# Inputs laid out in DRAM field by field, and two other weight chunks loaded in two parts, in a kernel of bilinear field pairs on one Trainium2 core

## Chip, core and metric

The kernel runs on one core of a Trainium2 chip (trn2). The metric is the time of one execution on the device in microseconds (us); of several executions the median is given. A profile shows one further execution, with what each engine did: PE is the matrix engine, PEld its weight loads, DVE, ACT and POOL are the vector, scalar and GpSimd engines, and SP is the sync engine, which here only issues DMAs. Sixteen DMA engines move all data between DRAM and the core's SBUF.

## The reference

There are 1024 samples of 32 fields, each a vector of 128 numbers, in float32. For each of the 496 pairs of fields i < j there is a 128 x 128 matrix of weights. The output of a pair is the vector of field i times the matrix, multiplied elementwise by the vector of field j:

```python
v_i = inputs[:, I_IDX, :]
v_j = inputs[:, J_IDX, :]
transformed = jnp.einsum('bpd,ped->bpe', v_i, W)
return transformed * v_j
```

The inputs are 16.8 MB, the weights 32.5 MB, the output is 260 MB.

## The kernel before

**Work and order.** The pairs are worked through with i falling from 30 to 0 (`_pairs`), so field 0 is needed last, and only as the left factor. A pair q has two halves of 512 samples; a unit u is one half of one pair. For each unit PE multiplies into a bank of PSUM (`first`, line 197), and DVE multiplies the result by x_j into an output tile `ot` (line 222). For float32 accuracy a product is made of three matmuls of split operands: of x_i the parts xh, xl, xd, of the weights wh, wl, wd. Two matmuls (line 207) are followed by a scaling on ACT (line 208), then the third (line 216). The first 15 pairs use the unsplit operands (line 204). Weights are split two pairs at a time, a "chunk of two" (`split_w`, lines 128 to 136): ACT makes wh (line 133), then POOL makes wl and wd in three instructions (lines 134 to 136). The fields are split in the same way by `split_x`. The list `todo` gives each split the pair from which it may run, some five pairs before its use.

The program's order on each engine is written out by hand: the loop over u at line 231 emits the instructions, and each engine runs its own in that order. An instruction that waits holds up what is behind it on its engine. SP has nothing to do but issue loads, so it is ahead of the others and waits only for what each load needs. POOL issues loads too, but between its splits, in its order.

**Buffers.** Weights are loaded eight pairs at a time, 512 KB: w_c is the c-th of 62 such chunks. Three buffers (tag "w") hold them in turn, so a load must wait until the splits of an older chunk are done. Field 0 (x_0) takes one turn of these three buffers, between w_54 and w_55, and so w_57 gets the buffer in which x_0 was, once POOL has split x_0. Chunk c is asked for at the pair `w_at` (lines 181 to 185): 17 pairs ahead of its first pair, but for w_55, w_56 and w_57, which are asked for 11 pairs ahead (`XAFTER`). Output tiles hold four pairs (2 MB) and there are three; ACT's queue issues their stores (line 255), and DVE waits for a store before it writes that buffer again.

**Loads in two parts.** Most loads are one DMA of 128 rows on SP. Some are in two parts (`load_apart`, line 107): 112 rows are one DMA that POOL issues, its access written with 14 as the outer size and 8 as the inner one, and the last 16 rows are one DMA that SP issues. `move_on(k)` (line 103) has POOL issue a tiny read of 2k pieces of 64 bytes into the tile `mark`, with k as the outer size: k is 5 ahead of all, 2 three pairs after each load in two parts, and 13 after the last of them. Loaded in two parts are the fields 1 to 14, two at a time (`load_x_apart`), and the weight chunks in `WAPART`. The host reorders the 112 rows of these so that each lands in its partition.

**Layout of x in DRAM.** `xt` is [128 dimensions, 32 fields, 1024 samples]: a row of a field is 4 KB, the next row of the same field lies 128 KB on. `wt` is [62, 128, 8, 128], each chunk one block of 512 KB.

Of the kernel before, what the change touches and what calls it, by code (L numbers as in the profile page):

```python
# [7 lines left out]
F32 = mybir.dt.float32  # L8
# [3 lines left out]
P = 128  # L12
NF = 32
NQ = NF * (NF - 1) // 2
BT = 1024
HB = 512
WC = 2
WL = 8
# [16 lines left out]
NE = 14  # L35
ROWS = 8 * NE
XAPART = 14
XSTEP, XPOS = 4, 8
WAPART = (45, 47, 49, 51, 54, 57, 59)
BACK = 3  # L40
SLAG = 2

# [7 lines left out]
def kernel(  # L50
# [22 lines left out]
    nc = tc.nc  # L73
# [3 lines left out]
    xpool = ctx.enter_context(tc.tile_pool(name="x", bufs=1))  # L77
    spool = ctx.enter_context(tc.tile_pool(name="xs", bufs=2))
    rpool = ctx.enter_context(tc.tile_pool(name="wr", bufs=WB))
# [3 lines left out]

    x_sb = {}

    def load_x(f, n=1, pieces=1, eng=None):

        if f == 0:

            t = rpool.tile([P, WL, P], F32, tag="w", name="x_0").rearrange("p q e -> p (q e)").unsqueeze(1)  # L90
        else:
            t = xpool.tile([P, n, BT], F32, tag=f"x{f}", name=f"x_{f}")
        s = BT // pieces
        for k in range(pieces):
            (eng or nc.sync).dma_start(out=t[:, :, k * s : (k + 1) * s], in_=xt[:, f : f + n, k * s : (k + 1) * s])
        for k in range(n):
            x_sb[f + k] = t[:, k, :]

    w_raw = {}

    mark = xpool.tile([32, 16], F32, tag="mark", name="mark")

    def move_on(k):

        nc.gpsimd.dma_start(out=mark[: 2 * k], in_=xt[: 2 * k, 0, :16].rearrange("(b a) n -> a b n", a=k))  # L105

    def load_apart(dst, src):
        nc.gpsimd.dma_start(out=dst[:ROWS], in_=src[:ROWS].rearrange("(b a) m n -> a b m n", a=NE))  # L108
        nc.sync.dma_start(out=dst[ROWS:], in_=src[ROWS:])

    def load_x_apart(f):

        t = xpool.tile([P, 2, BT], F32, tag=f"x{f}", name=f"x_{f}")
        load_apart(t, xt[:, f : f + 2, :])
        for k in range(2):
            x_sb[f + k] = t[:, k, :]

    def load_w(c, splits=(0, WL), eng=nc.sync):
        w_raw[c] = rpool.tile([P, WL, P], F32, tag="w", name=f"w_{c}")
        if c in WAPART:  # L120
            load_apart(w_raw[c], wt[c])
            return
        for a, b in zip(splits, splits[1:]):
            eng.dma_start(out=w_raw[c][:, a:b, :], in_=wt[c, :, a:b, :])
# [44 lines left out]

    load_w(0, (0, 1, WL), nc.sync)  # L170
    load_x(NF - 2, pieces=2, eng=nc.scalar)
    load_x(NF - 1, pieces=2, eng=nc.scalar)
    load_x(NF - 3)
    load_x(NF - 4)
    load_w(1, eng=nc.sync)
# [55 lines left out]
    for u in range(2 * NQ + LAG + SLAG):  # L231
        q = u // 2
        if u < 2 * NQ:
            i, j = pairs[q]
            if u % 2 == 0 and j == i + 1 and XAPART < i - 2 - XLEAD:
                load_x(i - 2 - XLEAD)
            first(u)
            if u == 2 * nq0:
                move_on(5)
            f = i - XSTEP  # L240
            if u % 2 == 0 and 0 < f < XAPART and f % 2 == 1 and j == i + XPOS:
                load_x_apart(f)
                back.append(q + BACK)
            if u % 2 == 1 and q in w_at:
                load_w(w_at[q])
                if w_at[q] in WAPART:
                    back.append(q + BACK)
            if u % 2 == 0 and q in back:
                move_on(16 - NE if q < w_q[WAPART[-1]] else 13)
            if u == 2 * x_at + 1:  # L250
                load_x(0)
# [43 lines left out]
```

## Time and profile before

| | |
|---|---|
| median of 5 runs | 753.18 us (752.01 to 755.11) |
| the profiled execution's time | 751.63 us |
| its span, first to last instruction | 749.9 us |
| granted clock of PE, mean | 0.992 |
| busy: PE, DVE, ACT, POOL | 93%, 86%, 84%, 81% |
| moved by DMA | 310 MB, 413 GB/s over the span |
| ACT's queue (q10: the stores) and SP's (q1: loads) | 82.7% and 13.1% of the 16 engines' time |
| loads that POOL issues (q0) | 9.64 MB, 3.6% |

How to read it: the page cuts the span into 40 slices of 18.75 us and gives each engine's busy tenths in each, and what the DMA engines moved. "A waits for B" is put down where an engine was idle before an instruction, to what released it. In a timeline line stand the start, the duration, the engine, the line of the code, the operation with its tiles, and in brackets the idle time before it and what ended that. An idle engine costs nothing unless another one, or the end, waits for it.

### The profile page before, as it was taken

The page shows a single profiled execution, that of the slowest core. Times are in us where ns is not written, and L with a number is a line of the kernel's source. Part 1 is how long each engine was busy: PE and PEld are TensorE (multiplying, and loading weights), DVE is VectorE, ACT ScalarE, POOL GpSimd, SP SyncE. Part 2 cuts the span into 40 slices and gives each one's busy share as a digit, 9 for nine tenths or more (in the row PEclk, how much of TensorE's full clock was granted, in tenths as well). Part 3 has the DMA queues.
Part 4 walks back from the last instruction along what each step waited for, and adds up shares of the span by engine and source line. Part 5 has one row for each costly group of instructions (what it writes and reads, how often), then busy time and mean ns, then how long its engine had stood idle before and what let it go on. Part 6 is the DMA issues. An engine that isn't in the chain of part 4 may idle for free.

```text
span 749.9 us, 11008 instructions
## 1 busy us (share of the span) xinstructions
PE 698.8 (93%) x2946; PEld 550.4 (73%) x2946; DVE 643.1 (86%) x1012; ACT 627.0 (84%) x1256; POOL 611.1 (81%) x892
## 2 busy tenths in 40 slices
PE   7989999998999999989999998999999999997994
PEld 3567777776777777768777776877787877776883
DVE  4989999998888888889979888988888888896995
ACT  1388889998898889889888988988898998876993
POOL 1888999999999998978988887888888878785671
PEclk9999999999999999999999999999999999998998
DMA  9999999999999999999999999999999999997998
GB/s 354 429 423 427 428 426 413 419 387 425 426 408 431 404 426 424 423 427 426 420 410 425 431 410 431 416 414 407 426 417 424 416 428 396 429 417 298 425 425 350
DMA packets 32957, 310.05 MB, mean 413 GB/s; under 512 B 4480, under 2 KB 4608, under 8 KB 16384
## 3 DMA queue, kind: packets, MB, share of 16 engines
q10 hardware_dynamic: 19584, 261.10, 82.7%
q1 hardware_dynamic: 10816, 38.61, 13.1%
q0 software_dynamic: 2496, 9.64, 3.6%
q8 instruction: 24, 0.39, 0.2%
q14 instruction: 37, 0.30, 0.1%
HBM read 49.29 MB, written 260.05 MB: 413 GB/s over the span
## 4 chain that ended last, share of the span: by engine, by line
PE 60%; DMA 20%; POOL 13%; DVE 4%; issue 2%; ACT 0%; DVEq 0%; POOLq 0%; ACTq 0%
PE po L207 38%; PE po L216 18%; DMA out_dram<-ot 18%; PE po L204 4%; DVE ot L222 3%; POOL wl L134 3%; POOL xd L154 3%; POOL xl L149 3%; POOL wd L136 2%; DMA w<-in_wt_dram 2%; POOL xl L150 1%; POOL wd L135 1%; DMA x<-in_xt_dram 0%; ACT wh L133 0%; DVE xd L262 0%
## 5 line engine op out<-in xcount | busy, mean ns | idle before, releaser
L222 DVE TENSOR_TENSOR ot<-po,x 128x512 f32<-128x512 f32 x992 | 628.6, 685 | 98.4 <-DMA out_dram<-ot 47.6
L208 ACT ACTIVATE po<-po 128x512 f32<-128x512 f32 x962 | 545.0, 583 | 86.3 <-PE po L207 34.5
L207 PE MATMUL po<-xl,wl 128*128 128x512 f32 x962 | 377.6, 393 | 15.4 <-POOL wl L134 15.3
L207 PE MATMUL po<-xh,wh 128*128 128x512 f32 x962 | 378.5, 393 | 11.8 <-DVE ot L222 11.6
L216 PE MATMUL po<-xd,wd 128*128 128x512 f32 x962 | 375.8, 391 | 9.6 <-ACT po L208 6.3
L134 POOL TENSOR_TENSOR wl<-w,wh 128x256 fp32r<-128x256 f32 x241 | 180.7, 750 | 55.6 <-ACT wh L133 53.2
L207 PEld LDWEIGHTS po<-xh,wh 128*128 128x128 f32 x962 | 180.9, 188 | 60.5 <-DVE ot L222 22.1
L207 PEld LDWEIGHTS po<-xl,wl 128*128 128x128 f32 x962 | 181.0, 188 | 59.7 <-POOL wl L134 23.6
L216 PEld LDWEIGHTS po<-xd,wd 128*128 128x128 f32 x962 | 181.0, 188 | 49.2 <-issue 5.9
L136 POOL TENSOR_TENSOR wd<-wl,wd 128x256 fp32r<-128x256 f32 x241 | 178.5, 741 | 20.1
L135 POOL TENSOR_SCALAR wd<-wh 128x256 fp32r<-128x256 f32 x241 | 99.3, 412 | 20.5
L133 ACT ACTIVATE wh<-w 128x256 fp32r<-128x256 f32 x241 | 99.3, 413 | 12.2 <-DMA w<-in_wt_dram 7.1
L149 POOL TENSOR_TENSOR xl<-x,xh 128x512 fp32r<-128x512 f32 x52 | 67.3, 1294 | 18.9 <-ACT xh L148 18.6
L154 POOL TENSOR_TENSOR xd<-xh,xl 128x512 fp32r<-128x512 f32 x32 | 41.3, 1292 | 2.7
L148 ACT ACTIVATE xh<-x 128x512 fp32r<-128x512 f32 x52 | 32.5, 628 | 11.3 <-DMA x<-in_xt_dram 11.1
L150 POOL TENSOR_SCALAR xl<-xl 128x512 fp32r<-128x512 f32 x52 | 34.7, 668 | 4.6
L204 PE MATMUL po<-x,w 128*128 128x512 f32 x60 | 27.9, 625 | 4.3 <-DMA x<-in_xt_dram 4.2
L204 PEld LDWEIGHTS po<-x,w 128*128 128x128 f32 x60 | 11.6, 198 | 19.8 <-issue 12.5
L262 DVE TENSOR_TENSOR xd<-xh,xl 128x512 fp32r<-128x512 f32 x20 | 17.7, 885 | 0.0
L105 POOL DMA_DIRECT2D mark<-in_xt_dram x15 | 9.6, 640 | 0.0
L108 POOL DMA_DIRECT2D w<-in_wt_dram x7 | 4.4, 624 | 0.0
L108 POOL DMA_DIRECT2D x<-in_xt_dram x7 | 4.4, 623 | 0.0
(5 smaller groups left out, 1.7 us busy)
## 6 DMA issues: line engine op xcount, KB each, us to landing
out_dram<-ot ACTq DMA_DIRECT2D x122, 2048.0 KB, 11.6
w<-in_wt_dram SPq DMA_DIRECT2D x54, 512.0 KB, 10.3
x<-in_xt_dram SPq DMA_DIRECT2D x16, 512.0 KB, 9.7
x<-in_xt_dram POOLq DMA_DIRECT2D x7, 896.0 KB, 13.8
w<-in_wt_dram POOLq DMA_DIRECT2D x7, 448.0 KB, 11.7
out_dram<-ot ACTq DMA_DIRECT2D x6, 512.0 KB, 8.0
x<-in_xt_dram ACTq DMA_DIRECT2D x4, 256.0 KB, 5.8
out_dram<-ot ACTq DMA_DIRECT2D x4, 256.0 KB, 6.0
```

The costliest lines, as they stand in the source:

```text
L133: nc.scalar.mul(h, raw, 1.0 - 2.0**-13)
L134: nc.gpsimd.tensor_tensor(l, raw, h.bitcast(F32), ALU.subtract)
L135: nc.gpsimd.tensor_scalar(d, h.bitcast(F32), EPS, 1.0, ALU.mult, ALU.mult)
L136: nc.gpsimd.tensor_tensor(d, l.bitcast(F32), d.bitcast(F32), ALU.subtract)
L149: nc.gpsimd.tensor_tensor(l, x_sb[f][:, s], h.bitcast(F32), ALU.subtract)
L150: nc.gpsimd.tensor_scalar(l, l.bitcast(F32), 1.0 / EPS, 1.0, ALU.mult, ALU.mult)
L154: nc.gpsimd.tensor_tensor(d, h.bitcast(F32), l.bitcast(F32), ALU.subtract)
L204: nc.tensor.matmul(po[u], w_raw[q // WL][:, q % WL, :], x_sb[i][:, s], start=True, stop=True)
L207: nc.tensor.matmul(po[u], w_s[c][t][:, r], x_s[i][t][:, s], start=t == 0, stop=t == 1)
L208: nc.scalar.mul(po[u], po[u], 1.0 + EPS)
L216: nc.tensor.matmul(po[u], w_s[q // WC][2][:, r], x_s[i][2][:, s], start=False, stop=True, skip_group_check=True)
L222: nc.vector.tensor_tensor(ots[g][:, k, s], po.pop(u), x_sb[j][:, s], ALU.mult)
```

## The change

The host lays x out as [32 fields, 128, 1024], a field being one block of 512 KB; the fields that are loaded two at a time lie as one block of 1 MB for both, with a row of 8 KB (both fields) for each dimension. The loads' access patterns follow. `move_on` reads its few short pieces from field 0. And in `WAPART` 57 and 59 are exchanged for 58 and 60.

```diff
-WAPART = (45, 47, 49, 51, 54, 57, 59)
+WAPART = (45, 47, 49, 51, 54, 58, 60)
...
-            (eng or nc.sync).dma_start(out=t[:, :, k * s : (k + 1) * s], in_=xt[:, f : f + n, k * s : (k + 1) * s])
+            (eng or nc.sync).dma_start(out=t[:, k * s : (k + 1) * s], in_=xt[f, :, k * s : (k + 1) * s])
...
-        nc.gpsimd.dma_start(out=mark[: 2 * k], in_=xt[: 2 * k, 0, :16].rearrange("(b a) n -> a b n", a=k))
+        nc.gpsimd.dma_start(out=mark[: 2 * k], in_=xt[0, : 2 * k, :16].rearrange("(b a) n -> a b n", a=k))
...
-        load_apart(t, xt[:, f : f + 2, :])
+        rows = xt[f : f + 2].rearrange("m d b -> (m d b)").rearrange("(d m b) -> d m b", m=2, b=BT)
+        load_apart(t, rows)
...
-    xt = _np.ascontiguousarray(x.transpose(2, 1, 0))
-    late = xt[:ROWS, 1 : XAPART + 1].reshape(NE, 8, XAPART, BT)
-    xt[:ROWS, 1 : XAPART + 1] = late.transpose(1, 0, 2, 3).reshape(ROWS, XAPART, BT).copy()
+    xt = _np.ascontiguousarray(x.transpose(1, 2, 0))
+    for f in range(1, XAPART, 2):
+
+        two = xt[f : f + 2].transpose(1, 0, 2).copy()
+        two[:ROWS] = two[:ROWS].reshape(NE, 8, 2, BT).transpose(1, 0, 2, 3).reshape(ROWS, 2, BT).copy()
+        xt[f : f + 2] = two.reshape(2, P, BT)
```

More of the change, by code (lines that the diff above doesn't have):

```diff
@@ L84, with load_x @@
     x_sb = {}
-    def load_x(f, n=1, pieces=1, eng=None):
+    def load_x(f, pieces=1, eng=None):
         if f == 0:
-            t = rpool.tile([P, WL, P], F32, tag="w", name="x_0").rearrange("p q e -> p (q e)").unsqueeze(1)
+            t = rpool.tile([P, WL, P], F32, tag="w", name="x_0").rearrange("p q e -> p (q e)")
         else:
-            t = xpool.tile([P, n, BT], F32, tag=f"x{f}", name=f"x_{f}")
+            t = xpool.tile([P, BT], F32, tag=f"x{f}", name=f"x_{f}")
         s = BT // pieces
         for k in range(pieces):
-            (eng or nc.sync).dma_start(out=t[:, :, k * s : (k + 1) * s], in_=xt[:, f : f + n, k * s : (k + 1) * s])
-        for k in range(n):
-            x_sb[f + k] = t[:, k, :]
+            (eng or nc.sync).dma_start(out=t[:, k * s : (k + 1) * s], in_=xt[f, :, k * s : (k + 1) * s])
+        x_sb[f] = t
     w_raw = {}
```

## The prediction, made before the changed kernel ran

> **What bounds the kernel now.** I read the page's slices first, then the waits of the stretch that stands out, then its timeline, then busy sums and DMA rates stretch by stretch. From the page:
>
> ```profile
> PE   7989999998999999989999998999999999997994
> DMA  9999999999999999999999999999999999997998
> GB/s 354 429 423 427 428 426 413 419 387 425 426 408 431 404 426 424 423 427 426 420 410 425 431 410 431 416 414 407 426 417 424 416 428 396 429 417 298 425 425 350
> ```
>
> The sixteen DMA engines are full from the first microseconds, at about 420 GB/s, and PE is nearly full too. Transfers are the tighter limit of the two. One slice of 18.75 us, the 37th (675 to 694 us), falls to 298 GB/s and to 7 tenths. Apart from the first and the last it is the only real hole. The waits from 660 us to the end:
>
> ```profile
> POOL wl L134 <- ACT wh L133: 18.1, 19, 5.8
> DVE ot L222 <- PE po L216: 7.4, 4, 6.0
> ACT wh L133 <- DMA w<-in_wt_dram: 6.6, 1, 6.6
> PE po L216 <- ACT po L208: 5.5, 1, 5.5
> ```
>
> One wait of 6.6 us of ACT for a weight load, and every other engine then waits 5.5 to 6 us for ACT. The timeline says which load:
>
> ```profile
> 663.94 0.74 POOL L134 TENSOR_TENSOR wl<-w,wh 128x256 fp32r<-128x256 f32 x1
> ...
> 665.93 0.62 POOL L108 DMA_DIRECT2D w<-in_wt_dram  x1
> ...
> 669.56 2.50 ACT L208 ACTIVATE po<-po 128x512 f32<-128x512 f32 x4
> ...
> 678.63 0.42 ACT L133 ACTIVATE wh<-w 128x256 fp32r<-128x256 f32 x1 [6.58 <-DMA w<-in_wt_dram]
> ```
>
> ACT is done at 672.05 and wants the first pair of w_57. Chunk 57 is loaded in two parts. SP issued its 16 rows at 657.92 (5.5 us to landing), as soon as the buffer was free; POOL's 112 rows stand in POOL's own order behind splits, and were issued only at 665.93; they took 12.5 us and landed at 678.5. ACT's queue is in order: the products of earlier pairs (L208) stand behind the waiting wh. What the stall costs, by stretches:
>
> ```profile
> core 0: us, PE busy (x) PEld busy (x) DVE busy (x) ACT busy (x) POOL busy (x), PEclk, DMA share, GB/s
> 678.00:683.00 5.00, 3.32 (x8) 2.67 (x9) 1.38 (x2) 3.66 (x8) 3.29 (x6) 0.50 0.31 129
> 683.00:686.00 3.00, 3.00 (x15) 2.40 (x13) 2.79 (x5) 2.41 (x6) 1.63 (x3) 0.96 0.87 360
> 686.00:690.00 4.00, 4.00 (x19) 3.34 (x18) 4.00 (x6) 3.61 (x8) 2.97 (x6) 1.00 1.12 326
> 690.00:726.00 36.00, 36.00 (x161) 29.80 (x160) 36.00 (x54) 33.45 (x68) 25.19 (x41) 1.00 1.00 421
> 726.00:738.00 12.00, 12.00 (x55) 9.93 (x54) 12.00 (x19) 10.82 (x21) 5.65 (x9) 1.00 0.94 393
> 738.00:748.00 10.00, 1.92 (x8) 1.03 (x6) 3.50 (x6) 1.17 (x3) 0.00 (x0) 0.83 0.99 397
> ```
>
> The last two columns are DMA share and rate. Transfers go on a while from what is queued, then run dry from 678 to 683 us. From 690 us PE and DVE never wait again, though DVE waited 8 times, 8.4 us in all, for stores between 560 and 665 us: the stall emptied the store queue (store landing 11.9 us median before it, 8.4 after).
>
> **The change part by part. (1) w_57 becomes one plain load on SP.** SP issues it where it now issues the 16 rows, at 657.92, since the wait is for the same buffer (which x_0 held until POOL had split it). Six plain weight loads issued between 560 and 670 us took 10.0 to 11.9 us. So w_57 lands at 667.9 to 669.8, 2.2 us or more before 672.05. The stall goes. For PE that is 5.5 us of idle, and the slow clock after it: in the chain of waits nine matmuls from 679.68 to 683.64 take 3.95 us, where nine take 2.04 us later (0.68 us for three), so 1.9 us more; 7.4 us in all. For the DMA, by bytes: 678 to 690 us moved 5 x 129 + 3 x 360 + 4 x 326 = 3.03 MB, which at the 421 GB/s of the next stretch takes 7.2 us, not 12: 4.8 us. In 726 to 738 us the queues were thin (393 GB/s): 4.72 MB at 421 take 11.2 us, another 0.8. DMA gains 5.6 us, PE 7.4. What is late next is the store queue, so the smaller one holds. Store waits of about 1 us come back (8.4/8), and while one lasts PE can be short of work when the queue is next free; I take off 0.6 us, about half of one. **Minus 5.0 us.**
>
> **(2) w_58 becomes a two-part load.** Its POOL issue (0.62 us, as now, only moved) comes one split of three instructions after w_57's place: 665.93 + 2.0 = 668.0. Queued behind it on POOL are the splits, delayed by what w_57's no longer costs, so nothing net. POOL's weight loads take 7.4/11.7/13.9 us (least, median, most), POOL's loads of both kinds at most 15.1. It lands at 679.7, at most 681.9. ACT wants it four pairs' cadence of 2.72 us after 672.05, at 682.9. Spare: 3.2 us, at least 1.0. Cost nothing; with 15.1 us it would be 0.2 us late. Its 16 rows on SP (7.1 us at most) are issued at about 662.7, where the full load is now.
>
> **(3) w_59 becomes plain, w_60 two-part.** w_59 is issued by SP at about 672 and wanted at 672.05 + 8 x 2.72 = 693.8: far ahead. w_60's POOL issue is 16 pairs after w_58's, 668.0 + 21.8 = 689.8, and wanted at 704.6: 14.8 us for a load of 11.7. Nothing, at most 0.3 us late with 15.1. The two kinds stay at seven loads each; the two tiny reads into mark (0.63 us of POOL each) only move along.
>
> **(4) Fields as blocks.** No instruction, byte or row length changes: a field still arrives in rows of 4 KB, a pair in rows of 8 KB; in DRAM a field's rows lie 4 KB apart, a pair's 8 KB, instead of 128 KB. The layout of before can be priced against w, which already lies in blocks. POOL's queue q0 carries only pairs of fields from 155 to 514 us, only weights from 516 to 700 us (besides the small reads):
>
> ```profile
> q0 software_dynamic: 1157, 6.18, 4.8%
> q0 software_dynamic: 1274, 3.26, 5.0%
> ```
>
> Columns: packets, MB, share of 16 engines. The first is 0.048 x 359 / 6.18 = 2.79 us per MB, the second 0.050 x 184 / 3.26 = 2.82. The 128 KB pitch costs nothing beside a block, so I take 0. Ends: x is 32 fields, 16.8 MB, 6.4 of them through q0. If all fell to the price of stores (q10 in the first stretch, 127.36 MB for 83.9%: 2.37 us per MB), q0's from 2.79 and the rest from 2.58 (q1 there, 16.54 MB for 11.9%), that would give 0.42 x 6.4 + 0.21 x 10.4 = 4.9 us. The other end: different addresses meet the stores worse, as from 686 to 690 us (share 1.12 for 326 GB/s, 3.4 us per MB): 0.65 x 6.4 = 4.2 us for the pairs alone.
>
> The Trainium skill, "DMA: Bandwidth & Descriptors", section "Latency and other measured facts", says that rows at a large power-of-two pitch copy slower (207 GB/s at 512 KiB against 214 in full, half at 4 MiB) and advises to lay tiles out contiguously; 128 KiB is not in its list. By its 3% (an estimate: 3% of 16.8 MB at 2.6 us per MB) 1.3 us more would be saved; the two q0 rows show nothing of it. The sum by the rule would be 746.9, by the rows 748.2.
>
> The sum is minus 5.0 us against the profiled execution's 751.63 us (span 749.9), so 746.6; that execution is 1.55 us below the median of the five runs, 753.18, and the same difference from the median gives **748.2 us**.
>
> **The rivals.** Within 0.3% of 753.18 means 750.9 to 755.4, about what a measurement of this kernel can tell from no change.
>
> A. The forecast: stall gone, DMA full to the end. 748.2, own range 746 to 750. Chance 0.60.
>
> B. The wait moves to the stores. Before the stall DVE waits 8.4 us per 105 us for stores; with the stall gone these waits last to the end: 8.4/105 x 65 = 5.2 us of PE's 7.4 come back. 753.2 - 2.2 = 751.0. For it: no store wait after 690 us now. Against it: DMA is full while DVE waits for it, so its idle 4.8 us can't be lost again unless bytes also move slower. Chance 0.15.
>
> C. Blocks read more cheaply too: 5.0 + up to 4.9, half of it likely: 745.7, at most 743.3. Against it: the equal q0 rows. Chance 0.13.
>
> D. Slower: block reads collide with the stores. Seven pair loads, each some 13 us, make 91 us at 419 GB/s now. If the rate there fell halfway to 326, to 372, it would cost 91 x (1 - 372/419) = 10.2 us: 758.4. It outweighs the gain from a rate below 396 on (5.0 us), and is slower by 0.3% below 386. For it: 326 GB/s occurs, from 686 to 690 us, beside a POOL load. Against it: that load was of weights in blocks just after the stall, and between the first slice and the stall no slice is under 387. Chance 0.07.
>
> E. The swap only moves the stall: w_58 or w_60 lands late. Each us late is a us lost; with both 1.5 us late 751.2. It needs over 16 us to landing, where 15.1 is the most. Chance 0.05.
>
> Faster by over 0.3%: A, C and part of B and E: 0.80; within 0.3%: most of B and E: 0.13; slower: 0.07. The range 743.5 to 751.5 reaches over B's 751.0 and C's far end, and leaves out D and the edges of B, C and E.
>
> **What would show it.** Right: no ACT wait for a weight load over 1 us after 660 us; w_57 issued by SP near 658 and landed before 671; no slice under 390 GB/s between 660 and 725 us; PEclk without its drop; store waits of DVE after 690 us, few. Wrong: an ACT wait near 683 or 705 us (E); store waits of 4 us or more after 672 (B); q0 from 155 to 514 us well off 2.8 us per MB (C below 2.6, D above 3.2); a slower first 30 us.

## The result, and the profile after

| | before | changed |
|---|---|---|
| median | 752.86 us (42 executions) | 748.93 us (23 executions) |
| the profiled execution's time, its span | 751.63, 749.9 us | 750.53, 748.7 us |

The times were taken anew side by side. The changed kernel is faster: ratio 0.9949, 95% interval 0.9937 to 0.9961, so 3.8 us gained (2.9 to 4.7). The ratio is worked out from all the executions and is not quite the quotient of the two medians, which are 3.9 us apart. A second comparison (after_again, below) gave 0.9934 (0.991 to 0.9957): 5.0 us by the ratio, 4.2 by the medians. The forecast was 748.2 us, 5.0 us gained.

From the page of the changed kernel, the busy tenths of PE and of the DMA engines and the rate, in slices of 18.7 us:

```profile
PE   7999999998999999999999999999999999999894
DMA  9999999999999999999999999999999999999988
GB/s 347 417 426 433 426 409 409 421 406 421 415 384 430 419 423 424 421 430 424 428 418 422 431 407 432 426 413 409 425 394 423 413 426 404 427 425 424 418 365 347
```

The hole in the 37th slice is gone: 424 GB/s, where it was 298. A smaller one is new in the 39th, 365 where it was 425. The waits from 660 us to the end of the changed kernel (engine and line, what it waited for: us in all, times, longest):

```profile
POOL wl L133 <- ACT wh L132: 15.7, 16, 4.9
DVE ot L221 <- DMA out_dram<-ot: 9.5, 7, 3.1
ACT po L207 <- PE po L206: 5.7, 6, 2.4
```

No engine waits for a weight load any more (lines have moved up by one: L132 is the wh of ACT). In its place stand DVE's waits for stores, 9.5 us, where before had none from 660 us on. One line of SP's timeline and one of POOL's, around chunk 57:

```profile
659.18 0.33 SPq L123 DMA_DIRECT2D w<-in_wt_dram  x1
```

```profile
669.20 0.62 POOL L106 DMA_DIRECT2D w<-in_wt_dram  x1
```

The first is w_57, now one load; it took 10.5 us and landed at 669.7. The second is POOL's part of w_58; it took 12.5 us and landed at 681.7, and ACT split its first pair at 684.1. Busy sums of the changed kernel by stretches (columns as in the prediction: DMA share and rate at the end):

```profile
678.00:690.00 12.00, 11.49 (x51) 9.18 (x50) 9.38 (x16) 10.31 (x22) 7.89 (x13) 1.00 1.01 426
690.00:706.00 16.00, 16.00 (x72) 13.15 (x71) 13.42 (x23) 14.62 (x30) 12.05 (x21) 1.00 1.01 416
706.00:712.00 6.00, 3.71 (x12) 2.59 (x11) 3.98 (x7) 2.34 (x5) 2.44 (x4) 0.78 1.01 431
712.00:718.00 6.00, 6.00 (x27) 4.87 (x25) 5.57 (x9) 5.11 (x11) 2.89 (x5) 0.94 0.73 309
718.00:738.00 20.00, 20.00 (x90) 16.52 (x88) 20.00 (x31) 18.14 (x35) 10.29 (x17) 1.00 0.92 386
```

From 678 to 690 us the DMA engines are full, where before they had a share of 0.72. Then something new: at 706 us PE stops and runs at a lowered clock, and at 712 us the DMA engines run short for 6 us. The chain of waits says from where (start, length, what):

```profile
693.79 14.10 DMA out_dram<-ot
...
708.01 0.70 DVE ot L221
...
708.76 0.77 PE po L206 x2
709.53 0.43 PE po L215
```

A store issued at 693.79 us took 14.1 us, the next one 14.0. They ran beside the loads of w_60 and w_61, which were both under way from 694.4 to 702.8 us. DVE had to wait for the buffer, PE for DVE, and then matmuls took twice their time (0.43 us where they take 0.23). How far the two kernels are apart on the way is read from ACT's first split of each chunk:

| first wh of | before | changed | gained |
|---|---|---|---|
| w_57 | 678.6 | 673.3 | 5.3 |
| w_58 | 690.3 | 684.1 | 6.2 |
| w_59 | 701.2 | 695.9 | 5.3 |
| w_60 | 712.1 | 706.8 | 5.3 |
| w_61 | 723.0 | 721.9 | 1.1 |
| end of the span | 749.9 | 748.7 | 1.2 |

The gain is there, 5.3 us, up to 707 us, and in this execution 4 us of it are lost at the new place. This execution is 1.6 us above the median of its kernel, the one of before 1.2 us below its own, so the median gain is larger than the two profiles show. Whether the new place belongs to the change is a question for the experiments.

### The profile page after: what moved, and what is told of

Its sections match the earlier page's. It is cut to its first block, busy times and chain, and to the rows that moved or that the text cites. A ratio compares the mean times of both kernels' runs of the same rounds, so it can differ in the third digit from the quotient of the medians.

```text
span 748.7 us, 11006 instructions
## 1 busy us (share of the span) xinstructions
PE 701.5 (94%) x2946; PEld 551.2 (74%) x2946; DVE 644.5 (86%) x1012; ACT 626.9 (84%) x1256; POOL 610.9 (82%) x892
## 3 DMA queue, kind: packets, MB, share of 16 engines
q1 hardware_dynamic: 10816, 38.61, 13.3%
## 4 chain that ended last, share of the span: by engine, by line
PE 54%; DMA 20%; POOL 15%; DVE 6%; issue 2%; ACT 1%; DVEq 0%; POOLq 0%; ACTq 0%
PE po L206 34%; DMA out_dram<-ot 19%; PE po L215 16%; DVE ot L221 5%; PE po L203 4%; POOL xd L153 4%; POOL wl L133 3%; POOL xl L148 3%; POOL xl L149 2%; POOL wd L135 2%; POOL wd L134 1%; DMA x<-in_xt_dram 1%; DVE xd L261 1%; ACT wh L132 0%; ACT po L207 0%
## 5 line engine op out<-in xcount | busy, mean ns | idle before, releaser
L132 ACT ACTIVATE wh<-w 128x256 fp32r<-128x256 f32 x241 | 99.2, 412 | 7.2 <-DVE ot L221 5.1
L203 PE MATMUL po<-x,w 128*128 128x512 f32 x60 | 30.1, 665 | 5.0 <-DMA x<-in_xt_dram 5.0
L203 PEld LDWEIGHTS po<-x,w 128*128 128x128 f32 x60 | 12.5, 213 | 21.8 <-issue 13.3
L261 DVE TENSOR_TENSOR xd<-xh,xl 128x512 fp32r<-128x512 f32 x20 | 19.1, 957 | 0.0
## 6 DMA issues: line engine op xcount, KB each, us to landing
w<-in_wt_dram SPq DMA_DIRECT2D x54, 512.0 KB, 10.4
x<-in_xt_dram SPq DMA_DIRECT2D x16, 512.0 KB, 10.2
w<-in_wt_dram POOLq DMA_DIRECT2D x7, 448.0 KB, 12.5
```

The source lines that it names most:

```text
L132: nc.scalar.mul(h, raw, 1.0 - 2.0**-13)
L203: nc.tensor.matmul(po[u], w_raw[q // WL][:, q % WL, :], x_sb[i][:, s], start=True, stop=True)
```

## The experiments

The theory: all of the gain is the exchange of w_57; the stall comes from POOL's place in its own order, and it costs what the DMA engines lose while dry. The rivals: the layout does a part (C, D); the two-part shape is itself what is late; the cost is the time that the engines wait; the new store waits take the gain back. Every kernel was run in turn with before on the same chip; ratios are to that, with 95% intervals.

**The exchange alone, in the layout of before (swap_only).**

```diff
-WAPART = (45, 47, 49, 51, 54, 57, 59)
+WAPART = (45, 47, 49, 51, 54, 58, 60)
```

> The kernel before with 58 and 60 for 57 and 59 alone; x stays at its 128 KB pitch. Theory (the exchange is the whole gain, the layout nothing): 0.995 of before, about 749 us, as the changed kernel; no wait of ACT for a weight load near 672 us. Rival (the blocks give part of it): 0.997 or more. Rival (the blocks cost something at the start, which hides part of the exchange's gain): 0.992 or less, first split of weights near 19.3 us as before, not 20.0.

749.01 us beside 753.48: 0.9931 (0.9915 to 0.9947). No wait for weights is left after 660 us, and the DMA share from 678 to 690 us is 1.01:

```profile
678.00:690.00 12.00, 11.28 (x50) 8.95 (x50) 9.74 (x17) 10.09 (x21) 7.74 (x13) 1.00 1.01 428
```

Within the intervals the exchange is the whole gain: 5.2 us by this ratio, 4.5 by the medians.

**The layout alone (layout_only).** The changed kernel with the chunks of before in two parts.

```diff
-WAPART = (45, 47, 49, 51, 54, 58, 60)
+WAPART = (45, 47, 49, 51, 54, 57, 59)
```

> The changed kernel with 57 and 59 put back; only the layout of x differs from before. Theory: 0.999 to 1.001, the 6 us wait for w_57 as before. Rival (blocks read more cheaply): 0.997 or less, with q0 between 155 and 514 us at 2.6 us per MB, not 2.8. Rival (blocks cost at the start): 1.002, with the full PE clock reached only near 13 us.

753.38 us beside 753.48: 1.000 (0.9985 to 1.0015). The stall is as it was, in the waits and in the stretch of this kernel:

```profile
ACT wh L132 <- DMA w<-in_wt_dram: 5.6, 1, 5.6
```

```profile
678.00:690.00 12.00, 8.60 (x28) 6.89 (x29) 5.86 (x9) 7.56 (x16) 6.17 (x10) 0.72 0.72 273
```

In all the layout brings nothing that can be told from 0 (0.15% either way); C and D fall. But two of its stages did change, in opposite directions. POOL's queue from 155 to 514 us carries the pairs of fields; in the changed kernel:

```profile
q0 software_dynamic: 1142, 6.07, 4.4%
```

That is 0.044 x 359 / 6.07 = 2.60 us per MB, where before had 2.79. Over the profiles, this queue takes 2.60 to 2.76 us per MB with pairs in blocks, 2.75 to 2.87 at the old pitch. The means of seven profiles each are 2.69 and 2.82: some 4%, 0.8 us of the loads' time. One profile alone can't show it: the weights on the same queue from 516 to 700 us, which are blocks in every kernel, took anything from 2.61 to 2.98. SP's queue from 0 to 27 us carries the first fields and weights; before and changed:

```profile
q1 hardware_dynamic: 2135, 7.30, 68.2%
```

```profile
q1 hardware_dynamic: 2031, 6.88, 66.2%
```

That is 0.682 x 27 / 7.30 = 2.52 us per MB, and by the same sum 2.60 in the changed kernel: here blocks are read a little slower, and ACT's first wh comes at 19.65 to 20.0 us with blocks, at 19.1 to 19.5 without. I had read the prediction's 0 as "no effect"; the stages show two effects of under 1 us with opposite signs. That the total is zero because they cancel is not shown (see hybrid below).

**w_57 loaded whole, no other put in its place (plain57), and w_58 alone put in its place (only58).** Both in the new layout. They ask whether the later two-part loads cost something.

```diff
-WAPART = (45, 47, 49, 51, 54, 58, 60)
+WAPART = (45, 47, 49, 51, 54, 59)
```

```diff
-WAPART = (45, 47, 49, 51, 54, 58, 60)
+WAPART = (45, 47, 49, 51, 54, 58)
```

> The changed kernel with 45, 47, 49, 51, 54 and 59 in two parts: 57, 58 and 60 all plain, 59 in two parts as before. Theory (in the changed kernel w_60 and w_61 are read together after 690 us, because POOL issues w_60 in its order; the stores behind them take 14 us, DVE waits 3 us, PE's clock halves): without that bunching no store wait over 2 us after 690 us and no second drop of the clock, 746 to 747.5 us, 0.992. Rival (the DMA is full, and the waits come back wherever the loads lie): 749, 0.995. Rival (the two-part loads themselves give time): slower than the changed kernel.

> The changed kernel with 45, 47, 49, 51, 54 and 58 in two parts; w_60 plain. Theory (bunching of w_60 and w_61 costs 2 to 3 us): 746 to 747.5 us, 0.992, w_60 issued by SP near 682 us and w_61 near 694, no store over 13 us to landing after 690 us. Rival (full DMA): 749, 0.995, with a store wait of 3 us somewhere after 684 us all the same.

plain57: 747.5 us, 0.992 (0.9902 to 0.9938), the figure of its theory, with no store wait over 1.3 us after 684 us. only58: 749.18 us, 0.994 (0.9923 to 0.9956), the figure of the rival. The intervals overlap with each other and with the changed kernel's. only58 has no store over 13.3 us, yet its DVE waits 7.1 us for stores after 672 us, nearly as long as the changed kernel (7.6). What these waits cost is seen from 690 to 738 us in only58:

```profile
690.00:738.00 48.00, 46.18 (x202) 37.39 (x200) 44.83 (x72) 41.38 (x82) 27.96 (x45) 1.00 1.00 421
```

PE and DVE idle here and there, but the DMA share is 1.00 at 421 GB/s (from 672 to 690 us 1.01 at 423): these waits cost no transfer time. So bunched loads as a standing cost of w_60 are not borne out.

**w_57 still in two parts, both issued by SP (sp57).** This tells the shape of the load from the place of its issue. (The edit also leaves out the tiny read that POOL issues three pairs after w_57.)

```diff
-    def load_apart(dst, src):
-        nc.gpsimd.dma_start(out=dst[:ROWS], in_=src[:ROWS].rearrange("(b a) m n -> a b m n", a=NE))
+    def load_apart(dst, src, eng=nc.gpsimd):
+        eng.dma_start(out=dst[:ROWS], in_=src[:ROWS].rearrange("(b a) m n -> a b m n", a=NE))
...
-            load_apart(w_raw[c], wt[c])
+            load_apart(w_raw[c], wt[c], nc.sync if c == 57 else nc.gpsimd)
...
-                if w_at[q] in WAPART:
+                if w_at[q] in WAPART and w_at[q] != 57:
```

> The kernel before, w_57 still in two parts with the same access patterns, but SP issues both. Theory (the stall comes from POOL's place in its order, not from the two-part shape): w_57 issued near 658 us and landed by 670, no wait at 672; 0.993 to 0.995, as the exchange. Rival (the 112-row load itself is slow, 12 us whoever issues it, or slower where SP issues it with 14 as outer size): landed after 672, a stall of some us left, 0.997 or more.

748.81 us beside 752.94: 0.9943 (0.9923 to 0.9963). The timeline of SP in this kernel:

```profile
659.76 1.00 SPq L108 DMA_DIRECT2D w<-in_wt_dram  x1
660.82 1.26 SPq L109 DMA_DIRECT2D w<-in_wt_dram  x1
```

The load has the same shape and is issued 6.2 us earlier than POOL did it (665.93), and no wait for weights is left. It was POOL's order, not the shape.

**A second stall (stall55).** w_55 in two parts instead of w_54, in before, so that two chunks are late.

```diff
-WAPART = (45, 47, 49, 51, 54, 57, 59)
+WAPART = (45, 47, 49, 51, 55, 57, 59)
```

> The kernel before with 55 in two parts in place of 54: a second chunk that is asked for only 11 pairs ahead. Theory: POOL issues it about 6 us before ACT wants it, it lands some 6 us late, a second stall: 757 to 759 us, 1.005 to 1.008. Rival (w_57's stall is particular to the buffer that x_0 held): no second stall, 753.

751.43 us: 0.9985 (0.9962 to 1.0009). My expectation fell: no loss can be seen (at most 0.7 us by the interval). The waits from 600 us on, and the stretches with and after the first of the two stalls:

```profile
ACT wh L133 <- DMA w<-in_wt_dram: 8.0, 2, 5.3
```

```profile
650.00:656.00 6.00, 4.35 (x19) 3.17 (x18) 4.59 (x8) 5.21 (x12) 4.37 (x6) 1.00 1.03 434
656.00:662.00 6.00, 4.92 (x22) 3.61 (x20) 5.22 (x8) 5.41 (x13) 5.66 (x8) 1.00 1.00 427
662.00:678.00 16.00, 13.44 (x58) 10.81 (x58) 12.94 (x19) 9.90 (x19) 12.31 (x21) 1.00 0.95 368
```

ACT waits 2.7 us for w_55 and 5.3 for w_57. During the first one and for six us after it PE loses time, but the DMA engines live on the stores that are queued: shares 1.03 and 1.00. A dip comes later, before the second stall begins at 674.1 us: 0.95 in the third stretch, and within it 0.86 from 662 to 668 us, 0.8 us of the engines' time. So the wait of 2.7 us emptied the queue for 0.8 us at most. That is against my own rival E as I priced it ("each us late is a us lost"). That w_54 is loaded whole here may have given something back; no run tells that apart.

**Two doses of the same stall (ask443, ask441).** In before, w_57 is asked for two or four pairs earlier (c is the chunk, `early` the pairs added to its lead of 11).

```diff
+        early = 2 if c == 57 else early
```

```diff
+        early = 4 if c == 57 else early
```

> The kernel before with w_57, still in two parts, asked for two pairs earlier: POOL issues it some 2 us earlier, near 664 us, and ACT waits about 4.5 us where it waited 6.6. Theory by engine time (each us of ACT's wait is a us of the end): 2 us gained, 0.997. Theory by transfers (a wait costs only the time for which the DMA engines run dry, which is the wait less some 2 us of stores still queued): 2 us gained too, but PE's slow clock may stay.

> The same, asked for four pairs earlier: POOL issues w_57 near 662 us, ACT waits about 2.5 us. Theory by engine time: 4 us gained, and 2.5 us less than the exchange gives: 0.997 to 0.998 if the exchange gives 0.994. Theory by transfers (a wait shorter than what the store queue holds costs nothing, as the wait of 2.7 us for w_55 in stall55 seems to have cost nothing): all of the exchange's gain, 0.993 to 0.995, no slice under 400 GB/s at 670 to 690 us.

ask443: 751.62 us, 0.9967 (0.9943 to 0.999). ask441: 748.17 us, 0.9917 (0.9886 to 0.9948). POOL issued w_57 8.2 us (ask443) and 10.2 us (ask441) before ACT wanted it, where in before it was 6.1. What was left of the wait, and the stretch 678 to 690 us of before, of ask443 and of ask441:

```profile
ACT wh L133 <- DMA w<-in_wt_dram: 4.8, 1, 4.8
```

```profile
ACT wh L133 <- DMA w<-in_wt_dram: 3.2, 1, 3.2
```

```profile
678.00:690.00 12.00, 10.32 (x38) 8.41 (x39) 8.17 (x12) 9.68 (x20) 7.89 (x13) 0.78 0.72 253
```

```profile
678.00:690.00 12.00, 8.30 (x30) 6.79 (x31) 6.46 (x11) 7.99 (x17) 6.19 (x11) 0.86 0.77 297
```

```profile
678.00:690.00 12.00, 12.00 (x47) 9.69 (x47) 10.80 (x16) 10.08 (x21) 8.97 (x15) 0.86 0.99 401
```

| | ACT's wait for w_57 | DMA share, 678 to 690 | ratio to before |
|---|---|---|---|
| before | 6.6 us | 0.72 | 1 |
| layout_only | 5.6 us | 0.72 | 1.000 |
| stall55 | 5.3 us, and 2.7 for w_55 | 0.71 | 0.9985 |
| ask443 | 4.8 us | 0.77 | 0.9967 |
| ask441 | 3.2 us | 0.99 | 0.9917 |
| swap_only | 0 | 1.01 | 0.9931 |
| sp57 | 0 | 1.01 | 0.9943 |
| changed | 0 | 1.01 | 0.9949, 0.9934 |

The time goes with the DMA column rather than with the wait. ask441 decides it: ACT still waits 3.2 us, PE stands idle for 2.2 us and its clock then drops (0.86, as in ask443), and yet it is as fast as the kernels without any wait; the 0.997 to 0.998 by engine time lie outside its interval. ask443 decides nothing, since both theories said 0.997; its profiled execution, 753.58 us, is also 2 us above its median. And the shares are those of one execution each. Counted by bytes, as the prediction did, ask441 should have lost something: from 660 to 690 us it moved 395 GB/s, 11.9 MB, where swap_only moved 12.7 (424 GB/s) and before 10.4 (346). The 0.8 MB less than swap_only are some 2 us, which the time does not show. So the time for which the DMA engines run dry fits better here than the bytes.

**Weights whole but for w_45 (weights_plain),** in before: are the two-part loads worth anything themselves?

```diff
-WAPART = (45, 47, 49, 51, 54, 57, 59)
+WAPART = (45,)
```

> The kernel before with all weight chunks but 45 loaded plainly; the pairs of fields stay in two parts. Theory (only w_57's lateness costs; otherwise one way of loading is worth the other): 0.992 to 0.994. Rival (two-part weight loads give time in themselves, by what they spare some DMA engines): 0.997 or more. Rival (POOL's issues and uneven loads cost): 0.989 or less.

750.07 us: 0.9961 (0.9942 to 0.998). There is no stall and the store waits are few, but it lies between the theory and the first rival. The nearest kernel is sp57, in the same layout and comparison: 0.9943 (0.9923 to 0.9963). The intervals overlap, so a worth of some 0.2% for the two-part weight loads is possible and not shown; plain57, of the other layout and another comparison, has 0.992.

**Pairs in blocks, single fields at the old pitch (hybrid),** with w_57 whole: the better half of each layout.

```diff
-WAPART = (45, 47, 49, 51, 54, 58, 60)
+WAPART = (45, 47, 49, 51, 54, 59)
...
-            (eng or nc.sync).dma_start(out=t[:, k * s : (k + 1) * s], in_=xt[f, :, k * s : (k + 1) * s])
+            (eng or nc.sync).dma_start(out=t[:, :, k * s : (k + 1) * s], in_=xt[:, f : f + n, k * s : (k + 1) * s])
...
-        load_apart(t, rows)
+        load_apart(t, xp[f // 2])
```

> w_57, w_58 and w_60 plain as in plain57, but single fields at the 128 KB pitch as before and only the pairs in blocks. Theory (two small effects of the blocks cancel: pairs read some 4% cheaper, 0.7 us in all, while at the start the plain fields arrive later, 0.7 us or more): 0.990 to 0.991, 1 us below plain57, with the first split of weights near 19.3 us and q0 below 2.75 us per MB from 155 to 514. Rival (both are chance of single executions): 0.992 as plain57, the first split anywhere from 19.3 to 20.

747.64 us: 0.9933 (0.9911 to 0.9955). First wh at 19.4 us and 2.69 us per MB on POOL's queue, so both halves are there, but the time is that of plain57: the rival, not the theory (0.990 to 0.991). Effects of half a us each can't be told in the total, so what the two halves are worth in time stays open.

**The changed kernel and plain57 once more, on one chip (after_again, plain57_again).**

```diff
-WAPART = (45, 47, 49, 51, 54, 58, 60)
+WAPART = (45, 47, 49, 51, 54, 59)
```

(The diff is that of plain57_again; after_again has no edit.)

> The changed kernel once more, for a second profile. Theory (the store wait of 3.2 us and the half clock at 709 us were one execution's): 0.994 to 0.996, store waits of 1 to 2 us after 684 us, no half clock there. Rival (they belong to the kernel): a store of 14 us to landing and the half clock again near 709 us.

> w_57, w_58, w_60 plain and only six chunks in two parts, once more, on the same chip as the changed kernel. If the first result holds (0.992): 747.5 us, 1 to 2 us below the changed kernel. If it was chance: the same as the changed kernel, 0.994 to 0.995.

after_again: 749.38 us, 0.9934 (0.991 to 0.9957). plain57_again: 747.70 us, 0.9913 (0.9879 to 0.9946). In after_again the stretch around 709 us looks like this:

```profile
706.00:712.00 6.00, 4.96 (x22) 3.82 (x21) 4.08 (x8) 4.39 (x10) 3.76 (x6) 1.00 1.01 431
```

No drop of the clock, and no store over 13.4 us. What the changed kernel showed at 709 us belongs to that execution and is no fixed part of the change. plain57_again is 1.7 us below after_again on the same chip, but the intervals overlap; that the chunks 58 and 60 in two parts cost a little is possible, not shown. plain57, hybrid and plain57_again have the lowest medians, all clearly faster than before, but their intervals overlap with those of the other kernels without the stall.

## Why the prediction was right

1. *The stall on w_57 goes because SP issues it.* Right. Issued at 659.18 (predicted 657.92), landed at 669.7 (667.9 to 669.8). swap_only and sp57 show that the issue's place in POOL's order was the cause of the stall; within their intervals no other part of the change is needed for the gain.
2. *w_58 lands in time.* Right: issued by POOL at 669.20 (predicted 668.0), landed at 681.7 (at most 681.9), wanted at 684.1 (682.9). It had 2.4 us to spare; 3.2 was predicted.
3. *w_60 lands in time.* Right: issued at 690.18 (689.8), landed at 702.8, wanted at 706.8: 4.0 us to spare. Rival E needed over 16 us to landing; 12.6 was the longest of the two.
4. *Blocks cost nothing and bring nothing.* Right in the sum (1.000, 0.9985 to 1.0015), not in its reason. I compared the pairs' rows at pitch with weights in blocks and found them equal, 2.79 and 2.82 us per MB; against the same pairs in blocks the pitch does cost some 4%. At the start, where I had not looked, blocks are the slower ones; that this makes up for it is argued and not shown. The rule of the Trainium skill, "DMA: Bandwidth & Descriptors", section "Latency and other measured facts", on rows at a large power-of-two pitch points the right way for the pairs, with about the 3% of its first figure; for SP's queue at the start (the first fields in rows of 4 KB, together with the first weights) this case shows the opposite, 2.51 to 2.54 us per MB at the pitch and 2.59 to 2.62 in blocks over all profiles. The 1.3 us that I had estimated from it did not appear in the time.
5. *The price is what DMA loses (5.6 us), not what PE loses (7.4).* Right in kind. ask441 kept 2.2 us of PE's idle and the slow clock after it and lost nothing that shows; stall55 added a stall and lost nothing that shows; ask443 kept some of the dry DMA time and some of the loss, but its interval (0.9943 to 0.999) is too wide to count. The size rests on bytes, and there ask441 does not fit.
6. *0.6 us off for the store waits.* If a term was mis-sized, it is this one. The first comparison measured 3.8 us (2.9 to 4.7) against the 5.0 forecast. The store waits did come back, as rival B said: 7.6 us after 672 us in the changed kernel, 5.9 in after_again, 2.3 to 7.1 in all other kernels without the stall, where B counted 5.2. B's price for them was wrong: DMA is full meanwhile (only58: 421 to 423 GB/s with 7.1 us of waits). The one place where they cost something is where DMA ran dry after the longest of them, at 712 us in the profiled execution, 6 x (1 - 0.73) = 1.6 us; from 690 to 738 us that execution had a DMA share of 0.94, after_again 0.99. How often that happens isn't known. By the ratios swap_only (5.2 us) and the second comparison (5.0) don't lack the missing 1.2 us, by the medians (4.5 and 4.2) they lack some of it, and the intervals of all three overlap: this stays open.

Of the signs that I had named for being right, those of the loads held: no wait of ACT for a weight load after 660 us, and w_57 issued and landed in time. Three others held only in part in the first profile, or not at all: DVE's store waits after 690 us were few, two, but 4.6 us long in all; PE's clock did drop; and of the slices from 660 to 725 us the last had 365 GB/s instead of 390. Two of the signs for being wrong came up as well. Store waits of 4 us or more after 672 us (B) were there; that sign was badly chosen, since it names waits of an engine that isn't the limit. A slower first 30 us was there too (ACT's first wh at 20.0 us instead of 19.3), and POOL's queue came to 2.60 us per MB, the edge of C's sign, both without an effect on the total that could be measured. What carries the account is not these signs but the loads' times and swap_only.

Two small slips of the prediction change nothing: the pair loads took 13.8 us in the middle rather than "some 13", which makes rival D's 10.2 us 10.8, and the time at which w_60 is wanted is 704.7 by its own sum, not 704.6.

## What to carry to other kernels

Where transfers are the limit, price a stall by how long the DMA engines run dry, that is by the wait less what is queued in front of them: here a wait of 3.2 us cost nothing that shows in the time, and one of 6.6 us some 4 to 5. A load that a busy engine issues is late by that engine's queue, so loads with little lead belong to an engine with nothing else to do. A change of layout is looked at stage by stage: behind a total of zero there were two small differences of opposite sign here, though neither could be told in the time.

## What the hardware showed that I had not expected

PE's clock can halve after an idle time of only about 2 us, and doesn't always. In the changed kernel PE was idle 2.29 us before 708.76 us, and the seven matmuls from 709.33 us on took 0.63 us each instead of 0.39. In the same execution it was idle 2.29 us before 181.47 us, and nothing followed; in layout_only it was idle 2.29 us before 180.62 us, and the clock halved. The stretch 181 to 184.5 us, the changed kernel first, layout_only second (PEclk is the third figure from the end):

```profile
181.00:184.50 3.50, 3.03 (x13) 2.53 (x14) 2.83 (x5) 2.17 (x4) 3.16 (x6) 1.00 0.99 421
```

```profile
181.00:184.50 3.50, 3.50 (x10) 2.71 (x9) 1.78 (x3) 1.75 (x3) 3.25 (x6) 0.51 1.01 431
```

Ten matmuls where there were thirteen, and the DMA share is the same. The low clock lasted 3.4 us in both places. Elsewhere it lasted 6.8 us, after 5.5 us of idle in before and after 3.05 in weights_plain (176 to 183 us: clock 0.51), but again 3.4 after 3.8 us in ask443, so the length of the idle time alone does not set it.

On the chip of after_again the median of the mean clock was 0.988 in before and 0.992 in the changed kernel, which fits one such period less of 6.8 us (0.5 x 6.8 / 750 = 0.0045). Slow executions of before do have the lower clock there (0.982 at 760.44 us, 0.994 at 750.28), and in the profiles above the low clock comes with the stalls. That the clock is not what costs is seen from ask441, and from one execution of before beside sp57: its mean clock was 0.941, and it took 753.10 us, no more than the median there (752.94).
